# A graph-attention kernel on one core: the same operations, issued in the order of another table of places

## The chip, the core and the metric

The kernel runs on one core of a Trainium2 chip. The metric is the device time of one execution in microseconds (us), median of several runs. A core has a matrix engine (TensorE, PE in the profile), a vector engine (VectorE, DVE), an activation engine (ScalarE, ACT), GpSimd (POOL) and SyncE (SP), which here only issues transfers. Each engine works through its own instructions in the order in which they were written, and waits on semaphores for the others and for transfers.

## The reference

A batch of 32 graphs with 512 nodes goes through a layer norm with a ReLU, and then through two graph-attention layers. The first has 4 heads of 256 features, the second one head of 512. The input is added at the end.

```python
h = jnp.maximum(_layernorm(x, axis=-1), 0.0)               # x: (32, 512, 512) float32
def gat_layer(x, mask, W, a_src, a_dst, bias, concat):
    xl = (x @ W).reshape(B, N, H, F)
    asrc = jnp.einsum('bnhf,hf->bnh', xl, a_src)
    adst = jnp.einsum('bnhf,hf->bnh', xl, a_dst)
    e = jax.nn.leaky_relu(asrc[:, :, None, :] + adst[:, None, :, :], NEG_SLOPE)
    e = jnp.where(mask[..., None], e, NEG_INF)
    attn = jax.nn.softmax(e, axis=1)
    out = jnp.einsum('bsdh,bshf->bdhf', attn, xl)
...
mask = (adj > 0) | jnp.eye(N, dtype=bool)[None]
h = jax.nn.elu(gat_layer(h, mask, W1, att_src1, att_dst1, b1, concat=True))
return x + gat_layer(h, mask, W2, att_src2, att_dst2, b2, concat=False)
```

## The kernel before

All matmuls are float32 and are done in blocks of 128 rows by some 256 columns, with seven products in place of eight for a 2 by 2 block multiplication (`sevens`, `sums1`, `sums2`). Three products are made for each graph: `project1` (nodes by W1), `gather1` (softmax weights by xl, per head) and the pair `project2` and `gather2` of the second layer. Products land in eight banks `mm`. ScalarE or VectorE copies or adds them out, and only then can the bank be written again. So a late copy holds TensorE up.

The softmax works in two passes. The source scores of the nodes are turned (`as<-z`, VectorE), written to memory in a small transfer (`das<-as`) and read back as rows spread over all partitions (`as<-das`, 512 KB; all three in `spread`). ScalarE makes `l<-as,z` from them, VectorE takes the masked minimum, ScalarE the exponential. The result goes the same way through memory (`drr<-rr`, `rr<-drr`), and the weights `p` are built from `rr`. The mask is added to `p` by GpSimd as an accumulating transfer (`p<-dm`). The mask itself is built from the adjacency (`m<-adj`), written out (`dm<-m`) and transposed by a transfer (`mt<-m`).

Every step is first recorded as a job of a `Program`: its engine, its cost, what it reads and writes, and the call that writes the instruction. `Program.order` then plays the whole program through once in a simple model of engines and of the two transfer queues, SyncE's and GpSimd's. Whenever an engine is free, the model starts the ready job of the lowest rank. The order in which jobs start is the order in which the instructions are written. The rank is `PLACES[v] / 100 + turn * i`: a table with one number for each job of the opening, of one pass of the loop and of the end. The loop over graphs has 31 passes, and all passes in the middle share the numbers of one (470 jobs). The model's transfers have a size in us (`XLOAD`, `ROWS` and others), a lead, a tail and a share of speed when both queues are busy (`DMA_LEAD`, `DMA_TAIL`, `SHARED`). Costs and transfer times of the model bear on nothing but the order.

In the profile L495 is every ScalarE operation (`act`), L498 every VectorE operation (`dve`), L501 the transfers of SyncE (`dma`), L506 those of GpSimd (`accumulate`) and L512 every matmul (`pe`).

Of the kernel before, what the change touches and what calls it, by code (L numbers as in the profile page):

```python
# [19 lines left out]
P = 128  # L20
# [24 lines left out]
class Banks(Slots):  # L45
# [172 lines left out]
)  # L218


class Program:
# [41 lines left out]
    def ranks(self):  # L263
# [5 lines left out]
        rank = []  # L269
# [90 lines left out]
def tile_gat(  # L360
# [1004 lines left out]
    LATE = 2  # L1365
# [325 lines left out]
```

## Time and profile before

| | before |
|---|---|
| median of 3 runs | 2783.66 us (2779.81 to 2785.59) |
| the profiled execution: its time, its span | 2778.11 us, 2776.3 us |
| PE busy | 2747.9 us (99% of the span) |
| DVE busy | 2561.7 us (92%) |
| ACT busy | 2224.7 us (80%) |
| POOL busy | 321.7 us (12%) |
| granted TensorE clock, mean | 0.998 |
| transfers | 502.15 MB, mean 181 GB/s |

The span lies 1.8 us under the profiled execution's own time. TensorE is the engine that sets the time. A wait on any other engine costs only what it passes on to TensorE.

### The profile page before, as it was taken

What the parts mean: (1) busy time and instruction counts of PE and PEld (TensorE: products, weight loads), DVE (VectorE), ACT (ScalarE), POOL (GpSimd) and SP (SyncE); (2) the same over time, 40 slices, a digit from 0 to 9 for tenths busy, and PEclk for the clock granted to TensorE, in tenths of its full rate; (3) what the DMA queues carried; (4) which work ended last, traced back from release to release, by engine and by line L of the source; (5) the groups of instructions that cost most, each with busy time, mean ns of one, the idle gap of its engine ahead of it and who ended that gap; (6) DMA issues with size and microseconds to landing.
All of it is one profiled execution on the core that took longest, in us unless ns stands there. A gap on an engine that the chain in (4) does not pass through costs nothing. (4 is left out here: it accounts for less than half of the span.)

```text
span 2776.3 us, 42499 instructions
## 1 busy us (share of the span) xinstructions
PE 2747.9 (99%) x12924; PEld 2375.5 (86%) x12924; DVE 2561.7 (92%) x6732; ACT 2224.7 (80%) x4907; POOL 321.7 (12%) x356
## 2 busy tenths in 40 slices
PE   7999999999999999999999999999999999999999
PEld 6688888888888888888888888888888888888887
DVE  7899999999999999999999999999999999999996
ACT  5978788788887787887888877878778788778783
POOL 0101111101111111111011111111111111101110
PEclk9999999999999999999999999999999999999999
DMA  7757766767666767667686666766666766677663
GB/s 224 182 146 180 199 177 173 199 172 201 175 179 180 187 177 199 178 175 195 170 206 174 175 184 174 191 190 176 178 194 172 203 173 172 194 168 201 165 159 117
DMA packets 375865, 502.15 MB, mean 181 GB/s; under 512 B 222804, under 2 KB 227668, under 8 KB 375636
## 3 DMA queue, kind: packets, MB, share of 16 engines
q1 hardware_dynamic: 329844, 332.68, 42.4%
q0 software_dynamic: 45792, 166.74, 25.1%
q8 instruction: 103, 1.69, 0.3%
q14 instruction: 126, 1.03, 0.1%
HBM read 316.41 MB, written 51.31 MB: 132 GB/s over the span
## 5 line engine op out<-in xcount | busy, mean ns | idle before, releaser
L512 PE MATMUL mm<-w_sb,hs 128*128 128x257 f32 (+3 forms) x2908 | 675.8, 368 | 12.8 <-ACT xl L495 5.9
L512 PEld LDWEIGHTS mm<-w_sb,hs 128*128 128x128 f32 x2908 | 540.1, 190 | 93.3 <-ACT xl L495 8.9
L506 POOL DMA_DIRECT2D p<-dm x314 | 273.5, 877 | 2328.9 <-DVE p L498 1095.2
L512 PE MATMUL mm<-w_sb,ht 128*128 128x258 f32 x2112 | 522.8, 382 | 0.1
L512 PE MATMUL mm<-p,xl 128*128 128x258 f32 (+1 forms) x1984 | 493.1, 383 | 1.5 <-ACT mm L495 0.8
L512 PE MATMUL mm<-w_sb,h 128*128 128x257 f32 x2056 | 487.2, 379 | 0.2 <-ACT mm L495 0.2
L498 DVE SCALAR_TENSOR_TENSOR p<-rr,z 128x512 f32<-128x512 f32 (+1 forms) x636 | 447.4, 742 | 4.6 <-DMA rr<-drr 4.4
L512 PEld LDWEIGHTS mm<-w_sb,ht 128*128 128x128 f32 x2112 | 394.5, 190 | 58.0 <-issue 0.7
L495 ACT ACTIVATE p<-p,z 128x512 f32<-128x512 f32 (+1 forms) x636 | 428.2, 713 | 19.6 <-DVE p L498 13.0
L512 PEld LDWEIGHTS mm<-w_sb,h 128*128 128x128 f32 x2056 | 389.3, 189 | 58.2 <-ACT mm L495 0.6
L512 PEld LDWEIGHTS mm<-p,xl 128*128 128x128 f32 x1984 | 365.1, 190 | 61.2 <-issue 5.5
L495 ACT ACTIVATE l<-l,low 128x512 f32<-128x512 f32 x516 | 369.7, 717 | 1.9 <-DVE low L498 1.6
L495 ACT ACTIVATE l<-as,z 128x512 f32<-128x512 f32 x516 | 353.2, 715 | 14.6 <-DMA as<-das 14.3
L498 DVE CUSTOM_DVE_ANT_1 l<-l,mt 128x512 f32<-128x512 f32 x516 | 345.3, 688 | 18.1 <-ACT l L495 12.7
L495 ACT ACTIVATE xl<-mm 128x258 f32<-128x258 f32 (+2 forms) x748 | 274.2, 376 | 81.5 <-PE mm L512 80.2
L495 ACT ACTIVATE mm<-mm 128x257 f32<-128x257 f32 (+2 forms) x498 | 169.8, 345 | 203.3 <-PE mm L512 108.4
L495 ACT ACTIVATE h<-mm,b_sb 128x256 f32<-128x256 f32 (+1 forms) x504 | 227.8, 473 | 121.5 <-PE mm L512 121.0
L512 PE MATMUL mm<-t,hs 128*128 128x258 f32 (+1 forms) x992 | 254.7, 380 | 0.0
L512 PEld LDWEIGHTS mm<-t,hs 128*128 128x128 f32 x992 | 183.6, 190 | 24.0 <-DVE xl L498 0.4
L495 ACT ACTIVATE xr<-h 128x512 f32<-128x512 f32 x256 | 159.7, 625 | 45.5 <-DVE h L498 42.8
L512 PE MATMUL mm<-xl,p 128*128 128x258 f32 (+3 forms) x752 | 190.0, 388 | 0.0
L498 DVE TENSOR_TENSOR xl<-xl,mm 128x258 f32<-128x258 f32 x372 | 155.7, 420 | 36.2 <-PE mm L512 31.7
(137 smaller groups left out, 3752.6 us busy)
## 6 DMA issues: line engine op xcount, KB each, us to landing
p<-dm POOLq DMA_DIRECT2D x314, 512.0 KB, 5.0
rr<-drr SPq DMA_DIRECT2D x159, 512.0 KB
x<-in_x_dram SPq DMA_DIRECT2D x129, 256.0 KB
adj<-in_adj_dram SPq DMA_DIRECT2D x128, 256.0 KB
as<-das SPq DMA_DIRECT2D x64, 512.0 KB
t<-in_x_dram SPq DMA_DIRECT2D x124, 256.0 KB
out_dram<-t SPq DMA_DIRECT2D x124, 256.0 KB
dm<-m SPq DMA_DIRECT2D x64, 256.0 KB
```

The costliest lines, as they stand in the source:

```text
L495: prog.add("ACT", cost, reads, writes, lambda: nc.scalar.activation(*a, **k))
L498: prog.add("DVE", cost, reads, writes, lambda: f(*a, **k))
L506: lambda: nc.gpsimd.dma_start(to, at, accum_op=OP.add), size,
L512: f(*a, **k)
```

## The change

The jobs, their dependences and their number stay the same (15064 jobs). What changes is the order in which they are written, by two edits. The planner's model of transfers becomes finer: each kind of transfer, told by its size, has a lead, a tail and two shares of speed of its own, the sizes are set anew, and a table `LATE` can add to the landing of a transfer at a place (it is empty here). And all 2374 numbers of `PLACES` are others, chosen for the mean end of runs of such a model in which transfers land late at random and hinder others.

```diff
 PLACES = (
-    -54128, -54128, -54128, -54317, -50216, -53799, -49031, -53371, -49031, -48940, -49031, -48940, -5322, 4139,
+    -21124, -21123, -21187, -21124, -19956, -19941, -19942, -21301, -19903, -19904, -18841, -19897, -6146, 6511,
...
 )
+LATE = {
+   
+}
...
-    DMA_LEAD, DMA_TAIL, AHEAD = {"SP": 0.45, "POOL": 0.42}, {'SP': 1.2, 'POOL': 1.15}, 3.5
-    SHARED = {0.93: (0.31, 0.7), 0.77: (0.43, 0.71), 2.32: (0.75, 0.31), 1.16: (0.75, 0.31), 1.25: (0.35, 0.57)}
+    AHEAD, MASK, OTHER = 3.5, (0.75, 1.84), 0.76
+    KIND = {
+        0.3: (0.39, 1.21, 0.1, 0.9),
+        0.76: (0.81, 1.62, 0.33, 0.64),
+        0.77: (0.44, 1.45, 0.2, 0.82),
+        0.9: (0, 1.72, 1.0, 0.41),
+        0.92: (0.48, 2.18, 0.24, 0.89),
+        0.94: (-0.2, 1.76, 0.21, 0.6),
+        1.09: (1.58, 1.56, 0.53, 0.59),
+        1.84: (0.48, 2.18, 0.24, 0.89),
+        2.23: (0.58, 1.62, 0.53, 0.4),
+    }
...
+    def kind(self, j):
+
+        if self.jobs[j][0] == "POOL":
+            return self.MASK
+        return self.KIND.get(self.jobs[j][4], self.KIND[self.OTHER])
...
-                speed["SP"], speed["POOL"] = self.SHARED.get(jobs[wires["SP"][0][0]][4], (0.4, 0.6))
+                speed["SP"], speed["POOL"] = self.kind(wires["SP"][0][0])[2:]
...
-                release(j, lambda s: event + self.DMA_TAIL[which])
+                release(j, lambda s: event + self.kind(j)[1] + LATE.get(self.place[j], 0) / 100)
...
-                wires[e].append([j, free[e] + self.DMA_LEAD[e], jobs[j][4]])
+                wires[e].append([j, free[e] + self.kind(j)[0], jobs[j][4]])
...
-    XLOAD, STORE, MASKS, TURN, MASK_OUT, SMALL_ONE = 0.93, 0.77, 2.35, 1.25, 0.8, 0.1
-    ROWS = {4: 1.16, 8: 2.32}
+    XLOAD, WLOAD, STORE, MASKS, TURN, MASK_OUT, SMALL_ONE = 0.76, 0.92, 0.77, 2.09, 0.94, 0.9, 0.3
+    ROWS = {4: 1.09, 8: 2.23}
```

The rest of the diff puts these sizes where the loads are recorded, and one matmul cost of the model goes from `w / 593` to `w / 576`. Lines of the changed file lie 19 further down: L514 is `act`, L520 `dma`, L531 `pe`, L751 the transposing transfer of the mask (L732 before).

What the new order moves is shown at three places. The first is in a middle pass of the loop, on ScalarE, where the first three `l` are made from `as_113`, which is the spread row of the scores of two heads. `mm_132` to `mm_139` are the eight banks. Before:

```order
L495 ACTIVATE h_82<-mm_136,b_sb 128x256
L495 ACTIVATE xr_97<-h_82 128x512
L495 ACTIVATE l_101<-as_113,z_126 128x512
L495 ACTIVATE l_99<-as_113,z_126 128x512
L495 ACTIVATE l_100<-as_113,z_126 128x512
L495 ACTIVATE xr_96<-h_82 128x512
L495 ACTIVATE xl<-mm_139 128x258
L495 ACTIVATE h_82<-mm_138,b_sb 128x256
L495 ACTIVATE mm_134<-mm_133 128x258
L495 ACTIVATE mm_137<-mm_135 128x129
```

And after the change:

```order
L514 ACTIVATE h_82<-mm_132,b_sb 128x256
L514 ACTIVATE h_82<-mm_138,b_sb 128x256
L514 ACTIVATE l_100<-as_113,z_126 128x512
L514 ACTIVATE l_101<-as_113,z_126 128x512
L514 ACTIVATE l_99<-as_113,z_126 128x512
L514 ACTIVATE mm_137<-mm_135 128x129
L514 ACTIVATE mm_134<-mm_133 128x258
L514 ACTIVATE xr_96<-h_82 128x512
```

The copy `xl<-mm_139` stood two rows behind the three `l`. It now stands ten rows behind the last of them, and the copy `mm_137<-mm_135` is the first behind them.

On TensorE the same stretch reads, before the change:

```order
L512 MATMUL mm_135<-w_sb,hs 128x129
L512 MATMUL mm_139<-w_sb,hx_86 128x129
L512 MATMUL mm_138<-p_102,xl 128x256 x2
L512 MATMUL mm_133<-w_sb,ht 128x258 x2
L512 MATMUL mm_135<-wx_85,hs 128x129
L512 MATMUL mm_139<-w_sb,hs_84 128x258 x2
L512 MATMUL mm_135<-w_sb,ht 128x258 x2
L512 MATMUL mm_133<-w_sb,hs 128x258 x2
```

And after it:

```order
L531 MATMUL mm_135<-wx_85,hs 128x129
L531 MATMUL mm_138<-p_102,xl 128x256 x2
L531 MATMUL mm_135<-w_sb,ht 128x258 x2
L531 MATMUL mm_134<-w_sb,ht 128x258 x2
L531 MATMUL mm_133<-w_sb,hs 128x258 x2
L531 MATMUL mm_135<-w_sb,hs 128x258 x2
L531 MATMUL mm_133<-w_sb,ht 128x258 x2
L531 MATMUL mm_139<-w_sb,hs_84 128x258 x2
```

The pair `mm_139<-w_sb,hs_84`, which needs bank 139 free, moved back by five pairs. The first pair behind the step `mm_135<-wx_85,hs` that needs a copy is now `mm_135<-w_sb,ht`, one pair further on; it needs `mm_137<-mm_135`.

The second place is SyncE's queue in the same pass, up to the transfer that brings `as_113`. `t_106` to `t_109` are loads of x for the sum at the end, `dm_121` is the store of half a mask. Before:

```order
L501 DMA dm_121<-m 128x1024
L501 DMA t_109<-in_x_dram 128x512
L732 DMA_TRANSPOSE mt_110<-m 128x8x128
L501 DMA drr_118<-rr_114 4x8x32
L501 DMA t_107<-in_x_dram 128x512
L501 DMA das_117<-as_113 4x8x32
L501 DMA rr_114<-drr_118 128x1024
L501 DMA as_113<-das_117 128x1024
L501 DMA t_106<-in_x_dram 128x512
```

And after the change:

```order
L520 DMA t_109<-in_x_dram 128x512
L751 DMA_TRANSPOSE mt_110<-m 128x8x128
L520 DMA drr_118<-rr_114 4x8x32
L520 DMA dm_121<-m 128x1024
L520 DMA t_107<-in_x_dram 128x512
L520 DMA das_117<-as_113 4x8x32
L520 DMA rr_114<-drr_118 128x1024
L520 DMA as_113<-das_117 128x1024
L751 DMA_TRANSPOSE mt_110<-m 128x8x128
```

The store `dm_121<-m` moved behind the transpose and `drr_118<-rr_114`, to four rows ahead of `as_113<-das_117`. The load `t_106` no longer follows `as_113` directly.

The third place is SyncE's queue in the opening. Its first rows, before:

```order
L501 DMA x_91<-in_x_dram 128x512
L501 DMA x_88<-in_x_dram 128x512
L501 DMA x_89<-in_x_dram 128x512
L501 DMA x_90<-in_x_dram 128x512
L501 DMA w_sb<-in_L_gnn_W_dram 128x2x256
```

And after:

```order
L520 DMA w_sb<-in_L_gnn_W_dram 128x2x256
L520 DMA x_90<-in_x_dram 128x512
L520 DMA x_88<-in_x_dram 128x512
L520 DMA x_91<-in_x_dram 128x512
L520 DMA x_89<-in_x_dram 128x512
```

One load of W1 now stands ahead of the four loads of x. Further on, where W2 is loaded (`128x4x256`), before:

```order
L501 DMA adj_95<-in_adj_dram 128x512
L501 DMA dm_121<-m 128x1024
L732 DMA_TRANSPOSE mt_111<-m 128x8x128
L501 DMA w_sb<-in_L_gnn_W_dram 128x4x256
L501 DMA x_88<-in_x_dram 128x512
L501 DMA w_sb<-in_L_gnn_W_dram 128x4x256 x3
```

And after:

```order
L520 DMA adj_95<-in_adj_dram 128x512
L520 DMA x_88<-in_x_dram 128x512
L520 DMA w_sb<-in_L_gnn_W_dram 128x4x256 x2
L751 DMA_TRANSPOSE mt_111<-m 128x8x128
L520 DMA dm_121<-m 128x1024
```

The first load of W2 now goes out ahead of the transpose `mt_111` and the store `dm_121`, and behind one load of x.

More of the change, by code (lines that the diff above doesn't have):

```diff
@@ L268, in ranks @@
         turn = sum(job[1] for job in self.jobs[first : first + each] if job[0] == "PE")
-        rank = []
+        rank, self.place = [], []
         for j in range(n):
@@ L276, in ranks @@
                 v, i = first + each + j - last, (last - first) // each + 1
+            self.place.append(v)
             rank.append(PLACES[v] / 100 + turn * i)
@@ L594, in weights1 @@
                     dma(
-                        XLOAD, (), [("w1", ix, k)], w1_sb[:, ix, k, :, 2:],
+                        WLOAD, (), [("w1", ix, k)], w1_sb[:, ix, k, :, 2:],
                         w1[row : row + P, :].rearrange("p (j c f) -> p c j f", j=H // 2, c=2)[:, c],
@@ L604, in scores1 @@
                 dma(
-                    0.75, (), [vk + ("v", a, j)], bc[:, 2 * a + j, :],
+                    XLOAD, (), [vk + ("v", a, j)], bc[:, 2 * a + j, :],
                     bass.AP(tensor=v.tensor, offset=v.offset + j * 2 * FH, ap=[[0, P], [1, 2 * FH]]),
@@ L631, in weights2 @@
             dma(
-                1.5, [("ht", 0, 0)], [("w2", ix)], w2_sb[:, ix, :, :M],
+                2 * WLOAD, [("ht", 0, 0)], [("w2", ix)], w2_sb[:, ix, :, :M],
                 w2[r * HF // 2 : (r + 1) * HF // 2, c * DO // 2 : (c + 1) * DO // 2].rearrange(
@@ L646, in weights2 @@
             lk, bc = ts_.take()
-            dma(0.75, (), [lk], bc, rows_of(v[0], P))
+            dma(XLOAD, (), [lk], bc, rows_of(v[0], P))
             for (r, c), ix in AT.items():
@@ L1080, in step @@
             pe(
-                akeys + bkeys + ([tk + (1,)] if q == 1 else []), [bk], w / 593,
+                akeys + bkeys + ([tk + (1,)] if q == 1 else []), [bk], w / 576,
                 [(mm, (to, a, b), dict(start=q in (1, 5), stop=True, skip_group_check=True))],
```

305 rows, old and new, of the table PLACES are left out of this document.

## The prediction

> **What bounds the kernel now.** I read the page's first part, then the busy times by stretch, then the waits of TensorE, then the order of time around the commonest wait and around the longest.
>
> ```profile
> PE 2747.9 (99%) x12924; PEld 2375.5 (86%) x12924; DVE 2561.7 (92%) x6732; ACT 2224.7 (80%) x4907; POOL 321.7 (12%) x356
> core 0: us, PE busy (x) PEld busy (x) DVE busy (x) ACT busy (x) POOL busy (x), PEclk, DMA share, GB/s
> 0.00:62.00 62.00, 47.79 (x210) 40.99 (x211) 48.64 (x202) 30.02 (x64) 2.91 (x8) 0.92 0.85 242
> 62.00:180.00 118.00, 117.20 (x491) 89.10 (x491) 106.69 (x290) 98.08 (x214) 17.23 (x19) 1.00 0.65 164
> 180.00:2580.00 2400.00, 2392.05 (x11378) 2087.94 (x11377) 2243.88 (x5838) 1971.89 (x4353) 283.01 (x308) 1.00 0.69 182
> 2580.00:2776.30 196.30, 190.83 (x849) 157.46 (x847) 162.51 (x403) 124.67 (x278) 18.60 (x21) 1.00 0.55 152
> ```
>
> TensorE has work in 2747.9 of 2776.3 us, and the change takes none of it away. So only the 28.4 us of idle time are to be had, and the time lost to a lower clock. By stretch the idle time is 62 - 47.79 = 14.2 us in the opening, 0.8 up to 180 us, 2400 - 2392.05 = 7.95 us in the 2400 us of the loop, and 5.5 us at the end. A perfect order of the loop would gain 8 us, 0.3%. On the other side nothing bounds a loss: a wait of 0.3 us in each of some 30 passes costs 9 us.
>
> ```profile
> PE mm L512 <- ACT x L495: 9.5, 1, 9.5
> PE mm L512 <- ACT xl L495: 5.9, 11, 1.2
> PE mm L512 <- DVE hs L498: 3.7, 1, 3.7
> PE mm L512 <- ACT mm L495: 3.5, 7, 1.1
> ```
>
> The columns are the total in us, the number of waits and the longest. Two single waits belong to the opening, 9.5 us until the first layer norm is done and 3.7 us for `hs`. The one wait that returns in the loop is for ScalarE's copy `xl`: 11 times, 5.9 us, 0.54 us each. That is most of the loop's 7.95 us. Around the longest of them SyncE, ScalarE and TensorE read:
>
> ```profile
> 1869.14 0.52 SPq L501 DMA_DIRECT2D das<-as  x1
> 1869.76 0.39 SPq L501 DMA_DIRECT2D rr<-drr  x1
> 1871.37 0.33 SPq L501 DMA_DIRECT2D as<-das  x1
> ...
> 1869.28 0.28 ACT L495 ACTIVATE mm<-mm 128x129 f32<-128x129 f32 x1
> ...
> 1877.97 1.95 ACT L495 ACTIVATE l<-as,z 128x512 f32<-128x512 f32 x3 [1.41 <-DMA as<-das]
> 1879.83 0.61 ACT L495 ACTIVATE xr<-h 128x512 f32<-128x512 f32 x1
> 1880.35 0.36 ACT L495 ACTIVATE xl<-mm 128x258 f32<-128x258 f32 x1
> ...
> 1878.26 1.03 PE L512 MATMUL mm<-w_sb,ht 128*128 128x258 f32 x4
> 1879.13 0.39 PE L512 MATMUL mm<-wx,hs 128*128 128x129 f32 x2
> 1880.76 1.14 PE L512 MATMUL mm<-w_sb,hs 128*128 128x258 f32 x4 [1.24 <-ACT xl L495]
> ```
>
> The read-back `as<-das` went out at 1871.37 and released ScalarE at 1877.97, 6.6 us later. ScalarE had waited 1.41 us. Then three `l`, one `xr` and the copy `xl` had to run before the bank was free, and TensorE stood 1.24 us. So the late party is a transfer; ScalarE only passes the delay on.
>
> **The change part by part.** *The row that waits.* Landing to bank was 1880.76 - 1877.97 = 2.79 us before. In the new order the first pair that needs a copy is `mm_135<-w_sb,ht`, and behind the three `l` stands only `mm_137<-mm_135`. That is 1879.83 - 1877.97 = 1.86 us for the three `l`, 0.28 for the copy, and some 0.05 to the matmul: 2.19 us. TensorE's work between the pair whose copy completes the scores and the row that waits is the same in both orders, 13 pairs and 7 single steps. So the transfer has 2.79 - 2.19 = 0.6 us more room. Of waits of 0.54 us on average, the longest 1.2, I leave 1.1 us out of 5.9: a gain of 4.8 us. The bounds are 5.9 us, and the loss under the second rival.
>
> *Other transfers of the loop.* The table moves nearly every job by a few rows, and each transfer gets another distance to its reader. The nearest rows are what ScalarE and VectorE now wait for:
>
> ```profile
> ACT l L495 <- DMA as<-das: 14.3, 15, 4.2
> ACT p L495 <- DMA p<-dm: 6.0, 9, 1.5
> ...
> DVE p L498 <- DMA rr<-drr: 4.4, 4, 3.1
> ...
> p<-dm POOLq DMA_DIRECT2D x314, 512.0 KB, 5.0
> rr<-drr SPq DMA_DIRECT2D x159, 512.0 KB
> dm<-m SPq DMA_DIRECT2D x64, 256.0 KB
> ```
>
> `p<-dm` has 314 transfers and 9 waits of ScalarE, `rr<-drr` 159 and 4 of VectorE. Both have room now, and part of it will have been spent. I take 1.5 us of new waits of TensorE, between 0 and the 5.9 us that the worst row costs now.
>
> *The opening.* These rows are TensorE, VectorE and SyncE there:
>
> ```profile
> 0.75 1.82 SPq L501 DMA_DIRECT2D x<-in_x_dram  x4
> 2.61 0.69 SPq L501 DMA_DIRECT2D w_sb<-in_L_gnn_W_dram  x1
> ...
> 44.02 1.14 PE L512 MATMUL mm<-w_sb,ht 128*128 128x258 f32 x4
> 48.87 2.09 PE L512 MATMUL mm<-w_sb,hs 128*128 128x258 f32 x4 [3.71 <-DVE hs L498]
> ...
> 43.96 0.42 DVE L498 SCALAR_TENSOR_TENSOR xr<-w_sb,t 128x256 f32<-128x256 f32 x1 [1.65 <-DMA w_sb<-in_L_gnn_W_dram]
> ...
> 47.92 0.29 DVE L498 TENSOR_TENSOR hx<-hs 128x128 f32<-128x128 f32 x1
> 48.13 0.68 DVE L498 TENSOR_TENSOR hs<-hs,ht 128x512 f32<-128x512 f32 x1
> ...
> L498 DVE CUSTOM_DVE_ANT_1 l<-l,mt 128x512 f32<-128x512 f32 x516 | 345.3, 688 | 18.1 <-ACT l L495 12.7 <-ACT h L495 1.6 <-DMA mt<-m 0.4
> L498 DVE BATCH_NORM_STATS2 stats<-x 128x6 f32<-128x512 f32 x128 | 88.1, 688 | 2.3 <-DMA x<-in_x_dram 2.3
> ```
>
> The load of W1 now ahead of x holds the queue 0.69 us, so the first matmul, which hangs on all four x, comes some 0.6 us late. That is paid back in the 3.71 us wait, which lasts until VectorE has made `hs` at 48.8. Ahead of `hs` VectorE loses its wait of 1.65 us for W2, since that load goes out a transpose and a store earlier, and gains net work: three operations of 0.69 us (one BATCH_NORM_STATS2, two masked minima `l<-l,mt`) come ahead of `hs`, and one masked minimum and the `hx` of 0.29 drop behind it, +1.1 us. With its own start 0.6 us later this is -1.65 + 1.1 + 0.6, about 0. Bounds are -1.65 (the wait goes, the rest is hidden in VectorE's other gaps) and +1.7. I take 0.
>
> *The end.* One row of the chain that ended last closes it:
>
> ```profile
> 2700.25 72.42 PE mm L512 x300
> ```
>
> The last matmul ends at 2772.67, so 3.6 of the end's 5.5 us lie behind it; the 1.9 us of waits may come and go. I take 0, within 1 us either way.
>
> The sum against the profiled execution is 2778.1 - 4.8 + 1.5 = 2774.8 us. The median of the runs is 2783.7, 5.6 us above that execution. If those 5.6 us are of another kind, the same difference gives 2783.7 - 3.3 = 2780.4. If they are the same late row (0.19 us in each of 30 passes), they add to its 5.9, some 0.38 us a pass, of which 0.6 us of room leaves perhaps 2 us: 2783.7 - 9.5 + 1.5 = 2775.7. I take 2777.5 between them, nearer the second, since the one returning wait of the trace is that row.
>
> **The rivals.** *The clock of the opening.* Behind the 3.71 us wait the clock is down:
>
> ```profile
> 45.00:48.90 3.90, 0.19 (x2) 0.03 (x1) 3.90 (x13) 2.57 (x8) 0.00 (x0) 0.87 1.06 375
> 48.90:58.60 9.70, 8.70 (x27) 7.10 (x28) 6.34 (x27) 4.47 (x12) 0.00 (x0) 0.52 0.67 148
> 58.60:70.00 11.40, 11.18 (x58) 9.76 (x57) 10.68 (x43) 10.48 (x28) 1.05 (x1) 1.00 0.20 71
> ```
>
> From 48.9 to 58.6 us the granted clock is 0.52, with TensorE busy for 8.7 us: 8.7 x 0.48 = 4.2 us lost. The 0.87 in the stretch ahead means that the clock fell (1 - 0.87) x 3.9 / 0.5 = 1.0 us before 48.9, so 2.7 us after the last matmul ended at 45.16. TensorE now comes to this wait 0.6 us later and VectorE at about the same time as before, so the wait may shrink to 3.1 us. If it gets under 2.7 us, the 4.2 us are gained too: 2773.3. The Trainium skill (TensorE: Matmul & The Clock Gate, "What's actually happening") says that the clock is halved after at least one idle window of about 3.4 us, and that the window runs free of the program. By that rule a wait of 3.1 us would keep the clock, and this rival would hold; here the clock fell 2.7 us into a wait, so the trace sets the point lower and I give it the smaller chance.
>
> *A store in front of the late row: slower.* `dm<-m` now goes out four rows ahead of `as<-das` and ahead of `rr<-drr` and `das<-as`. It moves 256 KB.
>
> ```profile
> 1862.00:1882.00 20.00, 18.76 (x94) 16.43 (x93) 18.71 (x53) 12.85 (x30) 2.59 (x3) 1.00 0.92 222
> ```
>
> At the 222 GB/s of this stretch, with the DMA engines 0.92 busy, that is 1.18 us. If the queue has no gap to hide it, `as<-das` lands up to 1.18 us later, against 0.6 us of room. The point from which it decides is 0.6 us. Taken at 0.9 us, halfway between the two, 0.3 us is left in each of 30 passes: +9 us, 2792.7. For it speaks the share of 0.92; against it, that `das<-as` must land before `as<-das` goes out (1869.14 to 1871.37), so the queue has gaps. The Trainium skill (DMA: Bandwidth & Descriptors, "Queues, rings and completion order") says that each DMA engine takes descriptors of a ring in order. By that rule the store is served first, whatever its urgency; the trace of before has no such row.
>
> *The waits only change places.* What the row gains is spent by `p<-dm` and `rr<-drr`, whose room shrank, at the 5.9 us upper bound: +1 us, or 2783 with the spread of the runs. For it speaks that the new table keeps no more idle time to give; against it, that only one row of the loop was short.
>
> **How the numbers follow.** A measurement of this kernel can tell about 0.2% (5.6 us) from no change: under 2778.1 is faster, over 2789.2 slower.
>
> Forecast, 2777.5 us, its own range 2773 to 2782: 0.40, of which faster 0.29, same 0.11. The clock stays up, 2773.3: 0.16, all but 0.01 of it faster. The waits change places, 2783: 0.18, of which same 0.15, faster 0.02, slower 0.01. The store in front, 2792.7: 0.26, of which slower 0.24, same 0.02. Together faster 0.46, same 0.29, slower 0.25. Cases of both signs hold much of the chance, so the range goes from 2767, the clock case with the bound of 5.9 us and a gain of the opening, to 2793, the slower case at its own value. What lies above is half of that case, 0.13, and below some 0.05.
>
> **What would show it.** In the waits of TensorE the row `<- ACT xl` should fall from 5.9 us to about 1, with no other row of the loop above 2 us, and the stretch 180 to 2580 should show less than 5 us of idle time (7.95 now). `ACT l <- DMA as<-das` may stay as it is, since ScalarE may wait where TensorE doesn't. If `as<-das` releases ScalarE later than now and a row `<- ACT mm` of several us appears, the store was in the way. The first matmul should start near 10.1 us and the granted clock of 48 to 59 us tells the clock rival. The forecast is wrong if the loop's idle time is not lower than 7.95 us.

## The result, and the profile after

The changed kernel takes 2768.88 us (median of 11 runs, 2763.43 to 2771.97) against 2778.89 for the kernel before in the runs beside it. The ratio is 0.9965, 95% interval 0.9952 to 0.9978: faster by 10.0 us. The profiled execution took 2769.33 us (2778.11 before), its span is 2767.6 us. Two of the runs told of below, one of the kernel before (4141 us) and one of `store_late` (4367 us), came at a mean granted clock of 0.65 and 0.62 and count in no comparison.

The page's first part and the busy times by the same four stretches as before (TensorE, weight load, VectorE, ScalarE, GpSimd, granted clock, DMA share, GB/s):

```profile
PE 2742.4 (99%) x12924; PEld 2371.8 (86%) x12924; DVE 2558.2 (92%) x6732; ACT 2229.1 (81%) x4907; POOL 313.1 (11%) x356
0.00:62.00 62.00, 47.45 (x220) 40.77 (x221) 50.44 (x208) 31.87 (x70) 2.86 (x8) 0.97 0.84 242
62.00:180.00 118.00, 118.00 (x502) 91.43 (x502) 107.80 (x296) 103.97 (x227) 18.05 (x19) 1.00 0.67 170
180.00:2580.00 2400.00, 2394.26 (x11389) 2088.43 (x11389) 2245.17 (x5845) 1969.68 (x4341) 274.98 (x310) 1.00 0.69 183
2580.00:2767.60 187.60, 182.67 (x818) 151.22 (x816) 154.76 (x385) 123.56 (x274) 17.19 (x20) 1.00 0.54 152
```

TensorE does 220 + 502 matmuls by 180 us, where it did 210 + 491. In the loop its idle time fell from 7.95 to 2400 - 2394.26 = 5.74 us. The waits of TensorE, then those of ScalarE for the spread row and for VectorE's `h`:

```profile
PE mm L531 <- ACT x L514: 12.1, 1, 12.1
PE mm L531 <- ACT mm L514: 5.8, 10, 1.2
PE mm L531 <- DVE hs L517: 1.3, 1, 1.3
...
ACT l L514 <- DMA as<-das: 30.7, 33, 2.3
ACT xr L514 <- DVE h L517: 5.1, 5, 1.3
```

The row `<- ACT xl` (5.9 us) is gone, `<- ACT mm` rose from 3.5 to 5.8. ScalarE waits twice as long for `as<-das` as before (14.3 us), and TensorE feels little of it. The last row is the one that I had not looked at; in the trace of before it is

```profile
ACT xr L495 <- DVE h L498: 42.8, 57, 1.2
```

One pass around the first copy behind the three `l`, ScalarE and TensorE, and the opening's wait for `hs` with the granted clock behind it:

```profile
1277.01 0.47 ACT L514 ACTIVATE h<-mm,b_sb 128x256 f32<-128x256 f32 x1 [0.23 <-PE mm L531]
1278.87 1.95 ACT L514 ACTIVATE l<-as,z 128x512 f32<-128x512 f32 x3 [1.38 <-DMA as<-das]
1280.72 0.52 ACT L514 ACTIVATE mm<-mm 128x129 f32<-128x129 f32 x2
...
1281.03 2.01 PE L531 MATMUL mm<-w_sb,ht 128*128 128x258 f32 x8
...
49.40 1.65 PE L531 MATMUL mm<-w_sb,hs 128*128 128x258 f32 x4 [1.32 <-DVE hs L517]
...
48.90:58.60 9.70, 8.56 (x36) 7.22 (x37) 8.18 (x39) 6.00 (x18) 0.00 (x0) 0.82 0.62 185
```

ScalarE now waits 1.38 us for `as`, and TensorE follows the copy without a wait worth a row (by its start it is 0.09 us late). The row that waits for `hs` starts at 49.40 us (48.87 before) after 1.32 us (3.71), and the clock behind it is 0.82 (0.52).

Idle time alone does not give the 8.8 us between the two profiled executions. So each matmul's start is compared with the start of the one before it: what lies above the usual distance of its width (110 ns for 128 columns, 111 for 129, 216 for 256 and 257, 217 for 258, 429 for 512) counts as lost, a halved clock with it, and the time up to the first matmul too. The time of TensorE lost, in us, by stretch (the column "low clock" has the time at a granted clock of 0.50 between 44 and 62 us; the 6.6 us of matmuls that `fill` adds count as lost):

```
               by 180   180-350  350-2580  from 2580   low clock
before          24.2       3.8      17.9        5.3       10.2
after           19.9       2.5      16.7        3.3        3.4
after_again     19.3       2.1      12.7        3.3        3.4
opening_new     19.7      11.1      20.0        4.7        0
loop_new        19.3       4.5      14.1        6.9        0
end_new         23.3       3.7      16.9        8.2        6.8
opening_160     20.2       2.2      20.9        3.7        0
rest_130        24.4       2.1      12.2        3.3        6.8
xl_copy_up      21.3       3.3      20.1        4.6        6.8
bank_copy_up    18.4       2.4      19.9        3.3        0
store_late      21.3       2.5      20.4        4.3        3.4
fill            26.6       2.4      15.3        3.8        0
x_first         18.1       1.8      12.9        3.3        0
stats_first     16.9       2.4      14.7        3.3        0
```

The span less the lost time is 2725.0 to 2725.3 us in each of the 14 traces, so the table leaves nothing out. Some 5.6 us of the column from 350 to 2580 us are the rounding of the usual distances, 0.5 ns for each of 10,600 matmuls, the same in every row.

One trace is one draw: with the same old opening five traces lie between 19.3 and 24.3, with the same old loop between 15.3 and 20.9. Only the end repeats, 3.3 in each trace that has the new one. Means over the traces that share an order in a stretch, without those that have a seam or a moved row in it (the kernels are told of below): by 180 us 21.9 old (the kernel before, `loop_new`, `end_new`, `xl_copy_up`, `store_late`), 19.5 new (both of the changed kernel, `bank_copy_up`, `opening_new`, `opening_160`); 180 to 350 us 3.0 and 2.2; 350 to 2580 us 18.2 (five) and 13.9 (six); from 2580 us 4.4 and 3.3. The differences, 2.4 + 0.8 + 4.3 + 1.1, make 8.6 us.

### The profile page after: what moved, and what is told of

Read it like the earlier page. It is cut to its first block, busy times and chain, and to the rows that moved or that the text cites. A ratio compares the mean times of both kernels' runs of the same rounds, so it can differ in the third digit from the quotient of the medians.

```text
span 2767.6 us, 42320 instructions
## 1 busy us (share of the span) xinstructions
PE 2742.4 (99%) x12924; PEld 2371.8 (86%) x12924; DVE 2558.2 (92%) x6732; ACT 2229.1 (81%) x4907; POOL 313.1 (11%) x356
## 5 line engine op out<-in xcount | busy, mean ns | idle before, releaser
L531 PE MATMUL mm<-w_sb,hs 128*128 128x257 f32 (+3 forms) x2908 | 667.0, 367 | 5.1 <-ACT mm L514 3.3
L531 PEld LDWEIGHTS mm<-w_sb,hs 128*128 128x128 f32 x2908 | 539.7, 190 | 87.7 <-ACT mm L514 6.7
L531 PE MATMUL mm<-w_sb,ht 128*128 128x258 f32 x2112 | 528.6, 382 | 2.7 <-ACT mm L514 2.5
L531 PE MATMUL mm<-p,xl 128*128 128x258 f32 (+1 forms) x1984 | 495.8, 383 | 0.1
L531 PE MATMUL mm<-w_sb,h 128*128 128x257 f32 x2056 | 477.8, 379 | 0.0
L517 DVE SCALAR_TENSOR_TENSOR p<-rr,z 128x512 f32<-128x512 f32 (+1 forms) x636 | 456.0, 742 | 2.4 <-DMA rr<-drr 2.4
L531 PEld LDWEIGHTS mm<-w_sb,ht 128*128 128x128 f32 x2112 | 393.7, 190 | 63.6 <-ACT mm L514 6.4
L514 ACT ACTIVATE p<-p,z 128x512 f32<-128x512 f32 (+1 forms) x636 | 433.4, 720 | 17.7 <-DVE p L517 12.4
L531 PEld LDWEIGHTS mm<-w_sb,h 128*128 128x128 f32 x2056 | 389.0, 189 | 58.4 <-ACT xl L514 0.5
L531 PEld LDWEIGHTS mm<-p,xl 128*128 128x128 f32 x1984 | 367.2, 190 | 52.7 <-issue 6.0
L514 ACT ACTIVATE mm<-mm 128x257 f32<-128x257 f32 (+2 forms) x498 | 169.8, 347 | 269.2 <-PE mm L531 236.2
L514 ACT ACTIVATE l<-as,z 128x512 f32<-128x512 f32 x516 | 354.4, 716 | 30.8 <-DMA as<-das 30.7
L514 ACT ACTIVATE l<-l,low 128x512 f32<-128x512 f32 x516 | 370.3, 721 | 7.6 <-DVE low L517 6.7
L514 ACT ACTIVATE xl<-mm 128x258 f32<-128x258 f32 (+2 forms) x748 | 269.3, 382 | 91.4 <-PE mm L531 89.8
L514 ACT ACTIVATE h<-mm,b_sb 128x256 f32<-128x256 f32 (+1 forms) x504 | 231.0, 480 | 77.3 <-PE mm L531 76.6
L531 PE MATMUL mm<-t,hs 128*128 128x258 f32 (+1 forms) x992 | 246.1, 380 | 0.0
L531 PEld LDWEIGHTS mm<-t,hs 128*128 128x128 f32 x992 | 185.8, 190 | 25.5 <-DVE t L517 0.2
L531 PE MATMUL mm<-xl,p 128*128 128x258 f32 (+2 forms) x752 | 189.7, 388 | 1.0 <-ACT h L514 0.6
L517 DVE SCALAR_TENSOR_TENSOR h<-xr,h 128x512 f32<-128x512 f32 x256 | 172.2, 683 | 6.1 <-ACT xr L514 6.1
```

What stands on the lines that cost most here:

```text
L514: prog.add("ACT", cost, reads, writes, lambda: nc.scalar.activation(*a, **k))
L517: prog.add("DVE", cost, reads, writes, lambda: f(*a, **k))
L531: f(*a, **k)
```

## The experiments: where the gain lies

*The changed kernel once more*, no edit.

> The changed kernel once more, beside the kernels of this set. If the ratio of the first comparison (0.9965) belongs to the change, it comes back within 0.9952 to 0.9978: some 2766 against the 2775 of the kernel before. If it came from the few runs of the kernel before that lay high (2780 to 2786 in three of eleven), it is nearer to 0.998, 2770. Its trace is a second draw of the changed opening, loop and end: first matmul at 12 us, hs wait under 2 us, 17 us of TensorE time above its pace from 350 to 2580 us.

2766.55 us, ratio 0.9962 (0.9950 to 0.9975). The gain belongs to the change. The loop's idle time is 2400 - 2396.62 = 3.4 us in this draw, and the row `<- ACT mm` is at 3.0:

```profile
180.00:2580.00 2400.00, 2396.62 (x11410) 2098.40 (x11409) 2250.01 (x5854) 1974.93 (x4352) 275.76 (x311) 1.00 0.68 183
...
PE mm L531 <- ACT mm L514: 3.0, 4, 0.9
```

*One stretch new, the others old*, cut by the jobs' numbers. In these kernels and all below the order is written out:

```diff
-        for j in self.order():
+        for j in ORDER:
             self.jobs[j][3]()
```

> The kernel before, with the jobs up to the end of the first pass in the new order and all others in the old one. By the two traces TensorE is 4.4 us ahead at 180 us although its first matmul starts 2.6 us later. If the opening stands by itself, the run is 4.4 us faster than the kernel before (2774.5 against 2778.9, ratio 0.9984). By the prediction, which put the opening at nothing, it is within 1 us. If the loop takes the lead back in waits (its transfers are then no earlier), also within 1 us, but with the stretch 48.9 to 58.6 us at a granted clock near 0.8.

> The kernel before, with only the passes of the loop after the first in the new order. By the two traces the loop's part is 2.4 us: 2776.5, ratio 0.9991, the wait for the copy xl gone and some 4 to 5 us of waits for ScalarE's copies between banks in its place. By the prediction it is 3.3 us, 2775.6. If the row xl had been the whole of it, it would be 5.9 us, 2773.0.

> The kernel before, with only the last three graphs' jobs in the new order. By the two traces the end's part is 2.0 us: 2776.9, ratio 0.9993. By the prediction it is nothing, 2778.9. If the three parts add, the gains of the three kernels sum to that of the whole change, 9.7 us; if they don't, a part is paid for in another.

Ratios 1.0009 (1.0000 to 1.0019), 1.0001 (0.9991 to 1.0011) and 1.0010 (1.0001 to 1.0020): no gain at all, each time. That is not what the parts are worth, but what the seams cost. In `opening_new` TensorE waits once, at 223 us, where rows of both orders meet:

```profile
222.96 2.08 PE L1350 MATMUL mm<-t,hs 128*128 128x258 f32 x4 [5.27 <-DVE t L1336]
```

`loop_new` loses 4.5 us from 180 to 350 us and 6.9 at the end, `end_new` 8.2 at its seam, against 2.2 to 4.4 without one. So these three decide nothing about the parts.

*A cut at a place where both orders have written nearly the same jobs*, 160 us in one direction and 130 us in the other.

> The new order up to 160 us and the old one from there; unlike in opening_new, the cut lies where both orders have written nearly the same jobs, so no seam of 5 us. Four traces with the old opening and four with the new one put the time that TensorE has lost by 180 us at 22.0 and 19.3 us. If the opening's part stands by itself, the run is 2.7 us faster than the kernel before, ratio 0.9990. By the prediction (nothing) it is 1.0000. If the old loop takes it back, also 1.0000, with the lead still there at 180 us.

> The reverse: the old order up to 130 us, the new one from there to the end. The traces put the rest at 1.1 us (180 to 350 us), 3.5 (350 to 2580) and 1.3 (the end): 6 us faster than the kernel before, ratio 0.9978. By the prediction's loop term alone it is 3.3 us, 0.9988. If the parts only work together, it is at 1.0000 like loop_new.

2773.91 us, ratio 0.9991 (0.9982 to 1.0000), and 2769.70 us, ratio 0.9980 (0.9970 to 0.9991). Both came as worked out from the traces. With 2775.8 for the kernel before they are 2.5 and 5.6 us, together 8.1 of the 10: the parts add within their intervals, and some 30% of it is the opening, the rest the loop and the end. The interval of `opening_160` reaches to nothing, though, so of the two only the gain of the rest is clear of noise.

```profile
62.00:180.00 118.00, 117.62 (x496) 90.54 (x495) 106.35 (x292) 99.51 (x216) 18.08 (x19) 1.00 0.65 170
180.00:2580.00 2400.00, 2391.72 (x11372) 2087.02 (x11371) 2243.71 (x5836) 1969.01 (x4345) 282.74 (x308) 1.00 0.68 182
...
PE mm L1350 <- ACT xl L1333: 6.6, 15, 0.7
```

These rows are `opening_160`: a loop with the old order has 8.3 us of idle time and the wait for `xl`, as before.

## The experiments: the row that waits

*The copy of the late row moved up, in the old order.* ScalarE, in each pass:

```diff
 l<-as_113,z_126
 l<-as_113,z_126
+xl<-mm_139
 l<-as_113,z_126
 xr_96<-h_82
-xl<-mm_139
```

> The kernel before with one row moved in each pass: ScalarE's copy xl, which stood behind the three l and one xr, now stands ahead of the third l. From the landing of as to the free bank there are then two l, the copy and 0.05: 1.23 + 0.28 + 0.05 = 1.56 us in place of 2.79, 1.2 us more room, more than any of the 11 waits but one. If the late transfer ahead of this row is what the loop loses, the wait for xl falls from 5.9 us to under 1 and the run is 5 us faster, ratio 0.998. If the waits only change places (the third l and the xr come 0.27 us later), the row falls but another rises by as much, ratio 1.000.

2778.45 us, ratio 1.0012 (1.0003 to 1.0021): slower. The wait for `xl` fell from 5.9 to 0.5 us as both theories had it, and another took its place, as the second had it:

```profile
PE mm L1350 <- ACT mm L1333: 5.2, 13, 0.9
...
PE mm L1350 <- ACT xl L1333: 0.5, 1, 0.5
```

One pass of it, ScalarE and TensorE:

```profile
1449.10 0.47 ACT L1333 ACTIVATE h<-mm,b_sb 128x256 f32<-128x256 f32 x1 [0.39 <-PE mm L1350]
1449.60 0.63 ACT L1333 ACTIVATE xr<-h 128x512 f32<-128x512 f32 x1
1450.65 1.34 ACT L1333 ACTIVATE l<-as,z 128x512 f32<-128x512 f32 x2 [0.41 <-DMA as<-das]
1451.89 0.36 ACT L1333 ACTIVATE xl<-mm 128x258 f32<-128x258 f32 x1
...
1453.64 0.54 ACT L1333 ACTIVATE mm<-mm 128x258 f32<-128x258 f32 x2
...
1453.02 1.03 PE L1350 MATMUL mm<-w_sb,hs 128*128 128x258 f32 x4
1454.23 1.14 PE L1350 MATMUL mm<-w_sb,ht 128*128 128x258 f32 x4 [0.18 <-ACT mm L1333]
```

The pair `mm<-w_sb,hs` at 1453.02 no longer waits. The next, `mm<-w_sb,ht`, needs `mm_137<-mm_135`, the second of the two copies at 1453.64, and is late. By the starts of the matmuls it is late in all 28 passes, 0.27 us each, 7.5 us. A transfer that is sometimes late cannot do that in each pass; a fixed row of steps can, and the moved copy lengthened it: in the 12 passes in which `as` is on time, ScalarE now waits 0.15 to 0.24 us in front of `xl` for TensorE's product, with the third `l` behind it.

*The same on the changed kernel*, where `mm_137<-mm_135` is the first copy behind the three `l`:

```diff
 l_100<-as_113,z_126
 l_101<-as_113,z_126
+mm_137<-mm_135
 l_99<-as_113,z_126
-mm_137<-mm_135
```

> The changed kernel with one row moved in each pass: ScalarE's copy between banks (mm_137<-mm_135), the first behind the three l, now stands ahead of the third l. In the changed kernel TensorE waits for it in 8 of the passes, 3.2 us. The copy then comes 0.6 us earlier and these waits go: 3 us faster than the changed kernel, ratio to the kernel before some 0.001 lower than that of the changed kernel. If the copy's own source is ready too late (the TensorE step ahead of it), ScalarE waits in front of the third l, VectorE's masked minima come later and it is as fast as the changed kernel or up to 2 us slower.

2772.00 us, ratio 0.9985 (0.9976 to 0.9994), 5.5 us slower than the changed kernel. It is the second case of the expectation:

```profile
1276.62 1.33 ACT L1333 ACTIVATE l<-as,z 128x512 f32<-128x512 f32 x2
1279.37 0.26 ACT L1333 ACTIVATE mm<-mm 128x129 f32<-128x129 f32 x1 [1.42 <-PE mm L1350]
1279.55 0.71 ACT L1333 ACTIVATE l<-as,z 128x512 f32<-128x512 f32 x1
```

ScalarE stands 1.42 us in front of the copy, whose source TensorE has not made, with the third `l` behind it. The waits for this copy go, and a pair four further on is late in all 28 passes, 0.2 us each, 5.7 us.

The medians over 26 passes, in us from the start of one earlier pair of TensorE (`mm<-p,xl`), the same in all four. The landing of `as` is read from the semaphore that the transfer counts up, over 28 passes:

```
                                    before  xl_copy_up   after  bank_copy_up
ScalarE's last step ahead of l ends   5.66        5.66    4.13          4.13
as lands                              5.73        5.75    5.10          4.84
first l starts                        5.73        5.74    4.99          4.86
third l starts                        6.98        7.41    6.23          7.10
copy mm_137<-mm_135 ends              9.27        9.44    7.19          7.18
pair that needs it starts             9.50        9.50    7.59          7.59
```

In the old order ScalarE comes to the first `l` just as `as` lands, and from there to the copy its rows are full, so there is no room for a late transfer. The medians hide what decides, and the single passes show it. In the kernel before there are 12 passes in which ScalarE did not wait for `as`, and in them TensorE is at most 0.05 us late at these pairs. In the other 16 ScalarE waited 0.08 to 1.41 us, and TensorE is late by just that wait and some 0.1 us more, 9.9 us in all. So the late party is the transfer. It is not VectorE's `h`, whose row of 42.8 us stands above. In each pass of before, ScalarE's rows ahead of `l` read like these:

```profile
1277.84 0.47 ACT L495 ACTIVATE h<-mm,b_sb 128x256 f32<-128x256 f32 x1 [1.36 <-PE mm L512]
1278.70 0.47 ACT L495 ACTIVATE h<-mm,b_sb 128x256 f32<-128x256 f32 x1 [0.39 <-PE mm L512]
1279.56 0.47 ACT L495 ACTIVATE h<-mm,b_sb 128x256 f32<-128x256 f32 x1 [0.39 <-PE mm L512]
1280.07 0.63 ACT L495 ACTIVATE xr<-h 128x512 f32<-128x512 f32 x1
1280.89 1.95 ACT L495 ACTIVATE l<-as,z 128x512 f32<-128x512 f32 x3 [0.20 <-DMA as<-das]
```

Of the steps just ahead of `l`, the `xr` that waits for VectorE's `h` (0.87 us a pass) stands further ahead, with five rows between, and behind it ScalarE waits for TensorE's products. The last of these waits is 0.39 us in each of the 28 passes, so what came before it holds nothing up. In the new order the steps ahead of `l` are others and end at 4.13 us, and `as` goes out 0.55 us earlier and lands at 5.10 us (4.84 in the second draw). TensorE is late at the first pair there only where ScalarE waited more than 1.28 us, in 8 of the 28 passes.

Summed over the 28 passes, from that pair `mm<-p,xl` to the ninth pair behind the step `mm<-wx,hs`, TensorE loses 7.2 to 12.2 us in six traces with the old order (before, `opening_new`, `end_new`, `opening_160`, `store_late`, `fill`; mean 9.5) and 2.3 to 5.5 us in six with the new one (both of the changed kernel, `loop_new`, `rest_130`, `x_first`, `stats_first`; mean 4.0). That 5.5 us is as much as the whole loop gains. The two moved copies lose 12.3 and 9.8 us, of which 0.34 and 0.32 us in every pass are the move's own price: the passes without a wait for `as` lose that too. What late transfers cost in `xl_copy_up` is the rest, some 2.9 us in place of 9.9, as the first theory had it.

*The store alone*, in the old order (SyncE, 28 passes):

```diff
-dm_121<-m
 t_109<-in_x_dram
 mt_110<-m
 drr_118<-rr_114
+dm_121<-m
 t_107<-in_x_dram
```

> The kernel before with one row moved in each of 28 passes: the store dm<-m now goes out behind the transpose and drr<-rr, three rows nearer to as<-das, as in the changed kernel. By the second rival as<-das lands up to 1.18 us later, the wait of TensorE for xl grows by more than the 0.1 us that a pass has left, and the run is 9 us slower or more, ratio 1.003. If the queue has gaps there (in the changed kernel as<-das takes a median of 5.0 us from issue to landing, 5.3 before), nothing changes: 1.0000, and the wait for xl stays near 5.9 us.

Ratio 0.9995 (0.9986 to 1.0004). No loss; the waits, with 5.9 and 14.3 us in the kernel before:

```profile
PE mm L1350 <- ACT xl L1333: 4.2, 12, 0.9
...
ACT l L1333 <- DMA as<-das: 11.8, 16, 4.6
```

From issue to landing `as<-das` takes a median of 5.5 us here, 5.3 before, 5.0 in the changed kernel. So the store in front of it does not hold it up by anything that the time shows.

## The experiments: the opening

*TensorE kept at work during its wait for `hs`*, in the old order. The added matmuls also change the product that their bank takes next.

```diff
+            if j == 326:      # the pair that waits for hs
+                self.fill()   # 30 x matmul(bank 5, identf, identf), 128 columns
             self.jobs[j][3]()
```

> The kernel before, with 30 matmuls of 128 columns on a constant put ahead of the TensorE row that waits 3.7 us for hs in the opening; their sums go to a bank that is free then and are overwritten later. They take 30 x 0.11 = 3.3 us of a wait of 3.7. If what the wait costs besides its own length is the clock, the granted clock stays near 1.00 from 48.9 to 58.6 us and 4 us are gained: 2774.9, ratio 0.9985. If TensorE's rows after the wait are late for other reasons (they wait on VectorE), nothing is gained: 2778.9. If the added matmuls push hs back, the run is up to 3 us slower.

Ratio 0.9996 (0.9986 to 1.0006). The clock stays up and the gain does not come, but this decides nothing about the clock's price, because the 30 calls took twice the time that was expected. TensorE, VectorE's `hs`, and the stretches:

```profile
45.72 6.86 PE L1662 MATMUL mm<-identf 128*128 128x128 f32 x60
52.42 1.04 PE L514 MATMUL mm<-w_sb,hs 128*128 128x258 f32 x4
...
47.13 0.68 DVE L500 TENSOR_TENSOR hs<-hs,ht 128x512 f32<-128x512 f32 x1
...
48.90:58.60 9.70, 8.70 (x61) 7.89 (x61) 5.08 (x21) 4.22 (x12) 0.00 (x0) 1.00 0.45 139
...
62.00:180.00 118.00, 115.38 (x479) 86.29 (x478) 105.84 (x288) 96.28 (x209) 15.98 (x19) 1.00 0.66 161
```

The trace has 60 matmuls, 6.7 us of them, and not 3.3. VectorE has `hs` ready at 47.81 us, and the pair that needs it starts at 52.42: some 4.5 us later than it could, about as much as the clock was to save. From 62 to 180 us TensorE is idle for 2.6 us where it was for 0.8 (117.20 of 118).

What the clock costs can be read from the other traces. In the stretches at a granted clock of 0.50 the distances of the matmuls add up to a loss of 3.7, 2.5, 2.3, 1.3 and 0 us in the five traces with the old opening, and of 1.6, 1.6 and three times 0 in the five with the new one. The difference of the means is 1.3 us, about half of the opening's 2.4. `loop_new`, with the old opening and no low clock, has lost 19.3 us by 180 us, no more than the new openings. And in 80 runs of the kernel before in the three later sets, the mean time is 2777.6 us at a mean clock of 0.998 (16 runs), 2775.5 at 0.999 (59) and 2772.5 at 1.000 (5). So the clock counts, but no run here changes the clock and nothing else.

*The loads of x first again*, in the changed kernel, then also *the end of the statistics ahead of the W1 steps* (SyncE, VectorE):

```diff
-w_sb<-in_L_gnn_W_dram
 x_90, x_88, x_91, x_89<-in_x_dram
+w_sb<-in_L_gnn_W_dram
...
+stats<-stats          (stats_first only)
 xr<-w_sb,p
 xr<-w_sb,p
-stats<-stats          (stats_first only)
```

> The changed kernel with the four loads of x ahead of the load of W1 on SyncE's queue, as before the change. If the first matmul sets what follows, the 2.6 us by which it came later are won: ratio 0.001 lower than the changed kernel's. If the opening is set by VectorE, which makes hs at 49 us whenever TensorE comes, TensorE starts near 10 us and waits 2 us longer for hs, 3.3 us, the clock falls as in the kernel before, and the run is as fast as the changed kernel or up to 3 us slower.

> The kernel x_first with one more row moved: on VectorE the step that ends the statistics of the layer norm, which stood behind two steps on W1 that wait 2.3 us for that load, now stands ahead of them. The first matmul then starts at about 9.4 us, 2 us earlier. If the start counts, the run is 2 us faster than x_first, ratio 0.9948. If VectorE makes hs at 49 us in any case, TensorE waits 3.3 us for it in place of 1.3, the clock is halved for 3.4 to 10 us, and the run is 1.7 to 4 us slower than x_first, 0.9961 to 0.9970.

2764.75 us, ratio 0.9955 (0.9943 to 0.9968), and 2764.97 us, ratio 0.9959 (0.9945 to 0.9972). Both medians lie some 1.7 us under the changed kernel's 2766.55, and the intervals overlap, so whether they beat it is open. The start does come earlier. These are VectorE and TensorE in `x_first`, then TensorE in `stats_first`:

```profile
9.43 0.42 DVE L1336 SCALAR_TENSOR_TENSOR xr<-w_sb,p 128x256 f32<-128x256 f32 x1 [2.30 <-DMA w_sb<-in_L_gnn_W_dram]
10.26 0.17 DVE L1336 SCALAR_TENSOR_TENSOR stats<-stats 128x4 f32<-128x4 f32 x1
11.33 2.82 PE L1350 MATMUL mm<-identf,x 128*128 128x128 f32 x12 [11.33 <-ACT x L1333]
48.92 1.14 PE L1350 MATMUL mm<-w_sb,hs 128*128 128x258 f32 x4 [1.32 <-DVE hs L1336]
...
9.61 2.82 PE L1350 MATMUL mm<-identf,x 128*128 128x128 f32 x12 [9.61 <-ACT x L1333]
47.67 1.14 PE L1350 MATMUL mm<-w_sb,hs 128*128 128x258 f32 x4 [1.32 <-DVE hs L1336]
```

The changed kernel starts 2.6 us later than the kernel before in the two profiled executions, and 1.6 us later on the mean (11.6 to 12.1 us in five traces with the new opening, 9.5 to 10.9 in seven with the old). Some 0.5 us of it is the load of W1 in front (11.9, the mean, to 11.33), the rest two steps on W1 that stand ahead of `stats` on VectorE and wait for their load. My expectation that `hs` is made at 49 us in any case fell: the wait stays 1.32 in all seven traces, and in `stats_first` its row comes at 47.67 us, where the five with the changed opening have it at 48.83 to 50.50. What is gained at the start shows at 180 us in `stats_first` (16.9 us lost, against 18.4 to 20.2 in these five) and hardly in `x_first` (18.1); at the end of the run `stats_first` had lost it again in its loop (14.7 against 12.9), within what such draws vary by.

## Why the prediction was right or wrong

*The size.* Forecast 2777.5 on a median of 2783.66, a ratio of 0.9978; measured 0.9965 and 0.9962. The difference of 6.2 us was 3.8 short. The other 4.8 us between 2777.5 and 2768.9 are the three runs of before that were shown: later ones lie lower, 2775 to 2776 in three sets of 21 to 35. Of the 6.2 only 3.3 is the sum of the terms. The rest came from taking half of the gap between median and profiled execution for more of the late row; the later runs don't bear that out, so this part came close by luck. By terms, 3.3 us stand against 8.6 in the traces.

*The row that waits, 4.8 us.* Right, with its mechanism: the wait went (5.9 to 0 us), the late party was the transfer, and the stretch behind the first `l` loses 5.5 us less. "0.6 us more room" comes out too. On the scale of the table, TensorE bore a landing up to 5.66 us before and up to 4.13 + 1.28 = 5.41 after, 0.25 us less, but `as` lands 0.6 to 0.9 us earlier, which leaves 0.4 to 0.6 us more room. What the prediction did not have is the other half: ScalarE's own rows were full, so one row alone could not be moved. `xl_copy_up` gave the row 1.2 us of room and gained nothing.

*Other transfers, 1.5 us.* Too much. The loop gained 5.1 us from 180 to 2580 us, so the other rows cost some 0.4. `<- ACT mm` rose by 2.3 us in one draw and fell by 0.5 in the other; of the 5.8 us, 2.0 in four waits are the pair behind `as` again, and no wait of TensorE names `p`. The sign "no other row of the loop above 2 us" did not hold, and "less than 5 us of idle time" held in one draw (3.4) and not in the other (5.74).

*The opening, 0.* The term that was mis-sized most: 2.4 us by the traces, 2.5 by `opening_160`, beyond the bound of 1.65. "Some 0.6 us late" was right for the load alone and missed the W1 steps on VectorE, 1.6 in all on the mean. "About 0" for `hs` was right, 48.87 to 49.40. So the wait shrank to 1.32, not 3.1.

*The end, 0 within 1.* 1.1 us, the steadiest part.

*The rivals.* The clock did stay up longer (3.4 us low in place of 10.2, in two of the changed kernel's draws), and by its own condition, a wait under 2.7 us, this rival came true. Its price was too high: some 1.3 us by the means of the traces, not 4.2, since the old opening does not always lose 10.2 us of clock and the new one sometimes loses 3.4. The store in front is refuted by `store_late`. "The waits only change places" is what happens to one row moved alone, twice shown, and not to the table as a whole.

## What to carry to other kernels

A wait names who came last. Whether that one is to blame shows when the passes are split by whether it was late: here the passes with the transfer on time lost nothing, and the others lost its delay and 0.1 us more. A median over all passes hides this. When one row is moved, its own price shows in the same way, in the passes that had no wait before. If these are late now, the engine's row of steps was full, and the steps ahead of it have to move. Parts of an order can be timed apart only if it is cut where both orders have issued the same work; a seam cost 2 to 8 us here, more than a part was worth. Where single traces of one order differ by 5 us in a stretch, compare several traces that share the order before a term is sized.

## What was not expected of the hardware

The halved clock comes in pieces of one length. From the granted clock by 1 us it lasted 3.4 us in three of these openings (both draws of the changed kernel, `store_late`), 6.8 in three, 10.2 in one, and 0 in seven. The changed kernel from 49.88 to 53.30 us, `xl_copy_up` from 48.84 to 55.66:

```profile
49.00:50.00 1.00, 0.60 (x3) 0.50 (x4) 1.00 (x6) 1.00 (x4) 0.00 (x0) 0.94 0.89 311
53.00:54.00 1.00, 0.97 (x6) 0.75 (x4) 0.00 (x0) 0.89 (x4) 0.00 (x0) 0.85 0.92 266
...
48.00:49.00 1.00, 0.83 (x3) 0.70 (x4) 1.00 (x7) 0.49 (x2) 0.00 (x0) 0.92 1.05 399
55.00:56.00 1.00, 1.00 (x5) 0.84 (x4) 0.63 (x4) 0.01 (x1) 0.00 (x0) 0.67 0.00 0
```

The same wait may cost it or not: waits of 1.97 us (`xl_copy_up`) and 1.98 (`loop_new`) cost 6.8 us and nothing; a wait of 1.32 with one of 0.5 shortly ahead cost 3.4 us in two traces and nothing in five. The Trainium skill (TensorE: Matmul & The Clock Gate, "What's actually happening") has a free-running window of about 3.4 us and says the clock is halved after at least one idle window. The traces agree with the length, and with chance in where it falls; they differ in that waits much shorter than the window were enough.
